# Queueing the merge and modulation steps behind the traced products, with ten weight rows ahead of the merges

## Chip, core and metric

The kernel runs on one NeuronCore of a Trainium2 chip. The metric is the device time of one execution in microseconds (us), shown as the median of several runs; lower is better. One execution was also recorded by the profiler, and all views of the trace come from that one. The engines are named as the profile names them: PE (matrix multiplication), PEld (its weight loads), DVE (vector), ACT (scalar and activation), POOL, and SP, which issues nearly all DMAs. "q" after a name (SPq) means the engine's queue of DMA issues.

## What is computed

One block of an adaptively modulated network on x of shape (4, 1024, 2048), all float32:

```
mod = silu(c) @ wmod                    # 2048 x (6*2048): sections sa, ca, ga, sb, cb, gb
ga, gb = sign(g) * max(|g|, 0.25)
h = layernorm(x) * (1 + ca) + sa
x = x + ga * (causal_conv(h, K) + D*h)  # K: a kernel of 2048 taps from a state-space model, by FFT
h = layernorm(x) * (1 + cb) + sb
x = x + gb * (h @ W.T + bias + sum_e coeffs[e]*scales[e] * (h @ A[e].T) @ Bf[e].T)
```

The reference convolves along the last axis with a 4096-point FFT.

## The kernel before, in words

The kernel has three stages. **Start (0 to about 100 us)**: two sections of the modulation and the table of the convolution kernel K are made. **Convolution (to about 940 us)**: x is taken in 16 groups g of two blocks of 128 rows (r = 0, 1). The convolution is a block-Toeplitz product, done with a three-product scheme ("families" f = 0, 2, 1) with operands split in two float16 parts (`kh`/`kl` and `h`). **Feed-forward (to the end)**: a 2 by 2 Strassen-Winograd product of seven terms, with W and the low-rank update merged beforehand into seven weight matrices `wcd` in DRAM.

In `conv_mm` (L552) the loops run over q = 0, 1 (halves of the output) and r = 0, 1. Each (q, r) does family 0 into a PSUM tile `ya` (pa, L582), ACT copies it to `qs` (L585; the pool has one buffer), family 2 goes into a second tile `yb` (pb, L587), DVE adds `qs` to it (L589), and family 1 accumulates into pa once more (L593), which DVE then multiplies by the gate (L597). A family is 12 products for q = 0 and 24 for q = 1. PSUM tiles come from a pool `acc` of five buffers (ACC = 5, L772), shared with the merges.

The inputs h of group g + 1 are prepared while group g is convolved: statistics on DVE (`stats`, L506), normalising on ACT (L528), transposes on PE into `tp` (L539), modulation on ACT (L542), split on ACT and DVE (L548, L549). After the convolution `conv_post` (L616) stores the rows to `x1d` and takes a second set of statistics. Group 0 is special: its gate is not there until late, so its outputs are gated afterwards in `conv_late` (L608).

Beside this, work that only the feed-forward stage needs is spread through the convolution in small **steps**. A generator `rest()` (L884) hands them out one at a time:

- **rows**: one row block of `wmod`, 1 MB, loaded by SP (`mod_load`, L314, a pool `wm` of three buffers) and multiplied on PE (`mod_mm`, L320, four float32 products, which the trace shows as 8 records named `modps`). Sections 4, 3 and 5 remain for this stage: each has 16 rows and a closing item, 51 items in all. A section's rows accumulate in one PSUM tile, from row 0 to row 15.
- **merges**: first `prep_lora` (L385), which loads A (2 MB, `la`), takes its norms on ACT, loads Bf (2 MB, `lb`) into the same buffer, scales it, and writes it as float16 pairs `lbh` (ACT, L423) and `lbl` (DVE, L424). Then 8 times `merge` (L429), each 15 steps: eight steps of six products `lps` on PE (L448), each with an addition to the loaded weights on DVE (L450), and seven steps of squares, scalings, splits and stores on ACT, DVE and SP (L453 to L495). That makes 121 merge steps.

`rest()` yields two merge steps (MR = 2), then one row, and so on; once the rows are through it still yields an empty step in their place. A last step folds scales (`fold_scale`, L895).

The order: `conv_mm` calls `tick()` after each family, and once more inside each q = 1 family after 12 of its 24 products (L574). So a group has 18 ticks, and a list `PLAN` (L775) says what each does: every tick has one "S", a call of `step()` (L927), which from g = 1 on takes one step from `rest()`. Group 1's first family ends with tick 1, and so on: ticks 1 to 3 belong to (q 0, r 0), 4 to 6 to (q 0, r 1), 7 to 12 to (q 1, r 0), 13 to 18 to (q 1, r 1). This is the order in which the instructions are *traced*. The order in each engine's queue is made afterwards, at build time, by the framework's scheduler: it simulates the engines with its own estimates and lets an instruction that it believes ready overtake earlier traced ones that it believes not ready. On the chip every engine then takes its queue as it stands. DMA issues stand in SP's queue in the same way.

Of the kernel before, what the change touches and what calls it, by code (L numbers as in the profile page):

```python
# [34 lines left out]
class Net:  # L35
# [516 lines left out]
    def conv_mm(self, pl, hs, xs, std, tick, early, out):  # L552

        nc, v = self.nc, self.nc.vector
        gv = None if early else self.gat.rearrange("p (j e t) -> p j e t", e=2, t=P)
        ys = [pl["y"].tile([P, D], F32, tag="y", name="y") for _ in range(2)]
        sums = [pl["sm"].tile([P, 2], F32, tag=f"sums{r}", name="sums") for r in range(2)]
        out[:] = ys, sums

        def family(ps, f, q, r, first):  # L560
            pf = ps.rearrange("p j t -> p (j t)")
            last = 4 * q + 3
            for i in range(last + 1):
                o = P * max(0, i - 4 * q)
                k0 = P * max(0, 4 * q - i)
                c = 2 * i + 2 - f
                h = hs[i // 2][:, :, 4 + i % 2, r] if f == 0 else hs[c // 4][:, :, c % 4, r]
                for x, z in ((0, 0), (0, 1), (1, 0)):
                    nc.tensor.matmul(  # L569
                        pf[:, o:512], h[:, x], self.kf[f][z][:, ds(k0, 512 - o)],  # L570
                        start=first, stop=(i == last and (x, z) == (1, 0)), skip_group_check=True,
                    )
                    first = False
                if i == 3 and q == 1:  # L574
                    tick()

        for q in range(2):
            for r in range(2):
                y = ys[r]
                yv = y.rearrange("p (j e t) -> p j e t", e=2, t=P)  # L580
                jj = slice(4 * q, 4 * q + 4)
                pa = self.acc.tile([P, 4, P], F32, tag="a", name="ya")  # L582
                family(pa, 0, q, r, True)
                qs = pl["q"].tile([P, 4, P], F32, tag="qs", name="qs")
                nc.scalar.copy(qs, pa)  # L585
                tick()
                pb = self.acc.tile([P, 4, P], F32, tag="a", name="yb")  # L587
                family(pb, 2, q, r, True)
                v.tensor_tensor(yv[:, jj, 1, :], pb, qs, ADD)  # L589
                if not early:  # L590
                    v.tensor_tensor(yv[:, jj, 1, :], yv[:, jj, 1, :], gv[:, jj, 1, :], MUL)
                tick()
                family(pa, 1, q, r, False)  # L593
                if early:
                    nc.scalar.copy(yv[:, jj, 0, :], pa)
                else:
                    v.tensor_tensor(yv[:, jj, 0, :], pa, gv[:, jj, 0, :], MUL)  # L597
                    self.residual(xs[r], ys[r], std[:, r : r + 1], sums[r], q)
                tick()
# [168 lines left out]


ORDER = (0, 4, 5, 1, 6, 2, 3)  # L770
MR = 2
ACC, TPS = 5, 2  # L772


# [20 lines left out]
def net(ctx: ExitStack, tc: tile.TileContext, io):  # L795
    nc = tc.nc
    k = Net(ctx, tc, io)
# [18 lines left out]
    def section(sec, pools):  # L816
        for q in range(16):
            if q == 0:
                k.mod_begin()
            k.mod_mm(k.mod_load(pools[q % len(pools)], sec, q), q)  # L820
            yield
        if sec == 0:
            k.sa = k.mod_column(msm, k.kpool, "sa", 0.0)
            k.hinv = k.fold_scale(msm, k.ca, k.sa, "fs1")
        elif sec == 1:
            k.ca = k.mod_column(msm, k.kpool, "ca", 1.0)
        elif sec == 2:
            k.gas, (k.gad,) = k.mod_gate(msm, "gad")
        elif sec == 4:
            k.cb = k.mod_column(msm, k.cst, "cb", 1.0)  # L830
        elif sec == 3:
            k.sb = k.mod_column(msm, k.cst, "sb", 0.0)
        else:
            _, k.gbd = k.mod_gate(msm, "gbd", io["bias"])
        yield
# [4 lines left out]
    def merges():  # L840
        k.prep_lora(pl["lora"], pl["mrg"])
        yield
        for c in range(HC):
            yield from k.merge(pl["lora"], pl["mrg"], c)

    mer = merges()
# [23 lines left out]
    n = 0  # L870
# [12 lines left out]
        pl[name] = pool(left, "p1" + name, bufs)  # L883
    def rest():  # L884
        mods = (x for sec in (4, 3, 5) for x in section(sec, (wmp,)))
        n = 0
        for _ in mer:
            yield
            n += 1
            if n % MR == 0:  # L890
                next(mods, None)
                yield
        for _ in mods:
            yield
        k.ginv = k.fold_scale(msm, k.cb, k.sb, "fs2", k.winv)  # L895
        yield

    fill = rest()
    p2l = ExitStack()
    pr, wc, lf = {}, {}, {}  # L900
# [15 lines left out]
    def early():  # L916
        right.close()
        for name, bufs in (("l", 8), ("t", 1), ("s", 1), ("x2", 1)):
            pr[name] = pool(p2, "p2" + name, bufs, "right")
# [5 lines left out]
        return k.left(pr, u, lf[u])  # L925

    def step():  # L927
        if g >= 1 and "l" not in pr and next(fill, 0) == 0:
            early()

    def post(g, r):
# [10 lines left out]
    for g in range(16):  # L942
# [5 lines left out]
        if g == 15:  # L948
            while "l" not in pr:
                step()  # L950
            load_w(0, ORDER[0])
            lgen = next_left(0)
        plan = iter(PLAN)

        def tick():
            for a in next(plan):
                if a == "S":
                    step()
                    take(lgen, 1)
                elif a == "O":  # L960
                    take(prs.pop(g), 1)
                elif a == "P" and g > 1:
                    post(g - 1, 1)
                elif a == "Q" and g:
                    done[g] = cur
                    post(g, 0)
                elif a == "T" and 0 < g < 15:
                    stats(g + 1)
                elif a == "N" and g < 15:
                    if g + 1 not in prs:  # L970
                        prs[g + 1] = prep(g + 1)
                    take(prs[g + 1], 1)
# [103 lines left out]
```

## Time and profile before

| | |
|---|---|
| runs of the kernel before | median 2165.51 us of 3 (2163.79, 2165.51, 2169.34) |
| the profiled execution | 2160.88 us, of which the span of the trace is 2159.1 us |
| PE | busy 2070.2 us, 96% of the span |
| DVE, ACT | busy 1273.2 us (59%) and 912.2 us (42%) |
| mean granted PE clock | 0.982 |
| DMA | 483.00 MB, mean 224 GB/s |

PE's time by form, from the page's groups: 5376 products of the feed-forward stage (`fX`, `fY`, `fZ`, L712) take about 1200 us; 3456 of the convolution (`ya`, `yb`, L569) about 950 us of counted time, records overlapping; 768 records of rows (`modps`, L322) 116.5 us; 384 of merges (`lps`, L448), 256 of them 87.2 us; the transposes (`tp`) the rest.

How to read the views: a line of the timeline gives the start, the duration, the engine, the line of the kernel, the operation, output<-inputs, how many instructions were taken together, and in brackets the idle time before it with what ended it. A line of the waits gives who waited for whom, the total in us, the number of times and the longest. A line of the windows gives for a stretch of time the busy us of each engine (with the number of instructions), the granted clock, the busy share of the 16 DMA engines and GB/s.

### The profile page before, as it was taken

The page shows a single profiled execution, that of the slowest core. Times are in us where ns is not written, and L with a number is a line of the kernel's source. Part 1 is how long each engine was busy: PE and PEld are TensorE (multiplying, and loading weights), DVE is VectorE, ACT ScalarE, POOL GpSimd, SP SyncE. Part 2 cuts the span into 40 slices and gives each one's busy share as a digit, 9 for nine tenths or more (in the row PEclk, how much of TensorE's full clock was granted, in tenths as well). Part 3 has the DMA queues.
Part 4 walks back from the last instruction along what each step waited for, and adds up shares of the span by engine and source line. Part 5 has one row for each costly group of instructions (what it writes and reads, how often), then busy time and mean ns, then how long its engine had stood idle before and what let it go on. Part 6 is the DMA issues. An engine that isn't in the chain of part 4 may idle for free.

```text
span 2159.1 us, 27722 instructions
## 1 busy us (share of the span) xinstructions
PE 2070.2 (96%) x11084; PEld 1020.6 (47%) x11084; DVE 1273.2 (59%) x2037; ACT 912.2 (42%) x1267; POOL 2.7 (0%) x12
## 2 busy tenths in 40 slices
PE   5696999999999999999999999999999999999999
PEld 1143554545445555654555555545444444444444
DVE  6537778887788877765666566565533323232323
ACT  1246666666667666654555454554200000000000
POOL 0000000000000000000000000000000000000000
PEclk8797999999999999999999999999999999999999
DMA  9987577876775442397556465465695545555542
GB/s 399 379 294 292 209 284 277 306 260 246 280 293 183 173 158 98 127 360 275 218 214 217 173 225 214 169 244 192 248 345 183 185 156 171 169 165 167 175 153 72
DMA packets 127130, 483.00 MB, mean 224 GB/s; under 512 B 13670, under 2 KB 13799, under 8 KB 96023
## 3 DMA queue, kind: packets, MB, share of 16 engines
q1 hardware_dynamic: 126464, 479.65, 61.7%
q8 instruction: 87, 1.43, 0.3%
q10 hardware_dynamic: 538, 1.59, 0.2%
q14 instruction: 41, 0.34, 0.0%
HBM read 325.89 MB, written 155.30 MB: 223 GB/s over the span
## 4 chain that ended last, share of the span: by engine, by line
PE 62%; issue 25%; DVE 7%; DMA 3%; ACT 3%; SPq 0%; POOL 0%; POOLq 0%; DVEq 0%; ACTq 0%
PE fZ L712 23%; PE fX L712 15%; PE fY L712 15%; PE ya L569 3%; PE tp L662 3%; PE yb L569 2%; PE modps L322 1%; DVE h L549 1%; ACT x L622 1%; DVE y L604 1%; ACT h L548 1%; DMA xo<-x1d 1%; DVE s4wr L177 1%; DMA w<-wcd 1%; DVE st L513 1%
## 5 line engine op out<-in xcount | busy, mean ns | idle before, releaser
L712 PEld LDWEIGHTS <-lf 128*128 128x128 f16 x5376 | 525.8, 98 | 620.2 <-issue 0.5
L712 PE MATMUL fZ<-w,lf 128*128 128x512 f16 x2304 | 514.0, 379 | 0.2 <-ACT p L720 0.2
L569 PEld LDWEIGHTS <-h 128*128 128x128 f16 x3456 | 319.7, 98 | 317.1 <-issue 69.1
L569 PE MATMUL ya<-kh,h 128*128 128x512 f16 (+3 forms) x1536 | 380.5, 328 | 8.2 <-ACT qs L585 5.1
L712 PE MATMUL fY<-w,lf 128*128 128x512 f16 x1536 | 343.1, 379 | 0.0
L712 PE MATMUL fX<-w,lf 128*128 128x512 f16 x1536 | 342.5, 379 | 0.0
L569 PE MATMUL ya<-kl,h 128*128 128x512 f16 (+3 forms) x768 | 251.5, 328 | 0.0
L731 DVE SCALAR_TENSOR_TENSOR xo<-xo,mv,gb 128x512 f32<-128x512 f32 x128 | 95.2, 750 | 248.7 <-DMA xo<-x1d 236.7
L569 PE MATMUL yb<-kh,h 128*128 128x512 f16 (+3 forms) x768 | 192.2, 326 | 0.0
L720 ACT COPY p<-fZ 128x512 f32<-128x512 f32 x64 | 37.3, 582 | 292.5 <-PE fZ L712 275.0
L322 PE MATMUL modps<-wm,sct 128*32 128x512 f32 x768 | 116.5, 677 | 43.1 <-DMA wm<-in_wmod 34.0
L664 ACT ACTIVATE gt<-tp,sb,cb 128x256 f32<-128x256 f32 x256 | 123.9, 570 | 63.7 <-PE tp L662 62.1
L720 ACT COPY p<-fX 128x512 f32<-128x512 f32 x32 | 18.7, 586 | 303.9 <-PE fX L712 240.2
L542 ACT ACTIVATE t<-tp,sa,ca 128x256 f32<-128x256 f32 x256 | 126.2, 565 | 32.3 <-PE tp L539 23.4
L549 DVE TENSOR_TENSOR h<-t,h 128x1536 f16<-128x1536 f32 x64 | 112.2, 1754 | 28.2 <-ACT h L548 27.7
L569 PE MATMUL yb<-kl,h 128*128 128x512 f16 (+3 forms) x384 | 125.2, 326 | 0.0
L548 ACT CAST h<-t 128x1536 f16<-128x1536 f32 x64 | 94.1, 1470 | 26.2 <-DVE t L547 26.2
L736 DVE TENSOR_TENSOR fin<-fX,gb 128x512 f32<-128x512 f32 x32 | 22.1, 692 | 125.8 <-PE fX L712 125.7
L448 PE MATMUL lps<-lbh,lac 128*128 128x512 f16 x256 | 87.2, 382 | 6.4 <-ACT lbh L423 5.1
L675 DVE TENSOR_TENSOR lf<-gt,lf 128x1024 f16<-128x1024 f32 x64 | 76.7, 1220 | 18.3 <-ACT lf L674 18.2
L513 DVE BATCH_NORM_STATS2 st<-x 128x6 f32<-128x512 f32 x128 | 83.3, 681 | 5.1 <-DMA x<-in_x 5.1
L539 PE MATMUL tp<-ident,x 128*128 128x128 f32 x512 | 73.0, 279 | 12.8 <-ACT t L542 6.9
(236 smaller groups left out, 1863.1 us busy)
## 6 DMA issues: line engine op xcount, KB each, us to landing
wm<-in_wmod SPq DMA_DIRECT2D x96, 1024.0 KB
lfd<-lf SPq DMA_DIRECT2D x112, 512.0 KB
lf<-lfd SPq DMA_DIRECT2D x112, 512.0 KB
x<-in_x SPq DMA_DIRECT2D x32, 1024.0 KB
x1d<-y SPq DMA_DIRECT2D x32, 1024.0 KB
x<-x1d SPq DMA_DIRECT2D x32, 1024.0 KB
xo<-x1d SPq DMA_DIRECT2D x128, 256.0 KB
out<-xo SPq DMA_DIRECT2D x128, 256.0 KB
```

What stands on the lines that cost most here:

```text
L322: self.last = self.nc.tensor.matmul(self.modps[32 * g : 32 * g + 32, :], self.sct[:, j].rearrange("p r b -> p (r b)"), w[:, ds(512 * g, 512)],
L448: nc.tensor.matmul(ps, la[:, x, k, h], y[:, k, osl], start=(n == 0), stop=(n == 5))
L513: v.bn_stats(st[:, q], xs[r][:, ds(512 * q, 512)])
L539: nc.tensor.transpose(tp[:, c, r], xs[r][:, ds(P * (4 * k + 2 * i + c), P)], self.ident)
L542: nc.scalar.activation(t[:, 2 * i + c], tp[:, c], AF.Identity, bias=self.sa[:, d, b : b + 1], scale=self.ca[:, d, b : b + 1],)
L548: nc.scalar.copy(h[:, 0], t)
L549: v.tensor_tensor(h[:, 1], t, h[:, 0], SUB)
L569: nc.tensor.matmul(pf[:, o:512], h[:, x], self.kf[f][z][:, ds(k0, 512 - o)], start=first, stop=(i == last and (x, z) == (1, 0)), skip_grou ...
L664: nc.scalar.activation(t[:, c0 + c], tp[:, c], AF.Identity, bias=self.sb[:, c0 + c, b : b + 1], scale=self.cb[:, c0 + c, b : b + 1],)
L675: v.tensor_tensor(hl[:, :, 1, :], s, hl[:, :, 0, :], SUB)
L712: nc.tensor.matmul(ps[name], lf[i][:, k, x, :], wc[i][k // 4][:, k % 4, y, :], start=(first and n == 0), stop=(n == 3 * HC - 1), skip_grou ...
L731: v.scalar_tensor_tensor(x, x, m, self.gbias[:, h], ADD, ADD)
```

## The change

Three edits. (1) `conv_mm` keeps the last traced product in `self.cv`. (2) `step()` takes its step inside `tc.issue_after(k.cv.ins)`: each instruction of the step that runs on PE gets an edge that puts it behind that product in PE's queue. It is an order of issue alone, with no semaphore; instructions of the step on DVE, ACT, SP and POOL get no edge. When there is a step and when `early()` is called stays as it was. (3) `rest()` begins with ten rows of section 4 (MOD0 = 10), with `prep_lora` after the first two of them; and then one row follows each three merge steps instead of each two (MR = 3).

```diff
@@ family() in conv_mm, L568
                 for x, z in ((0, 0), (0, 1), (1, 0)):
-                    nc.tensor.matmul(
+                    self.cv = nc.tensor.matmul(
@@ L771
-MR = 2
+MR, MOD0 = 3, 10
@@ rest(), L884
         mods = (x for sec in (4, 3, 5) for x in section(sec, (wmp,)))
+        for n in range(MOD0):
+            if n == 2:
+                next(mer)
+                yield
+            next(mods)
+            yield
         n = 0
         for _ in mer:
@@ step(), L927
-        if g >= 1 and "l" not in pr and next(fill, 0) == 0:
+
+        with tc.issue_after(k.cv.ins):
+            more = g == 0 or "l" in pr or next(fill, 0) is None
+        if not more:
             early()
```

## Prediction

> **What bounds the kernel now.** I read the page's slices first, then the windows, then PE's timeline in the worst window, then its waits, and last SP's queue there. The slices:
>
> ```profile
> PE   5696999999999999999999999999999999999999
> ...
> PEclk8797999999999999999999999999999999999999
> ```
>
> From slice 5 on PE is busy nine tenths or more: PE sets the time, and a change that keeps PE's work (this one removes no product) can only gain idle PE time or lost clock. Idle time stands mainly in slices 1 to 4. The windows show what of it lies where this change reaches, from g = 1 on (about 167 us):
>
> ```profile
> 160.00:180.00 20.00, 17.86 (x116) 9.83 (x114) 18.02 (x25) 13.08 (x19) 0.00 (x0) 1.00 0.96 379
> 180.00:200.00 20.00, 2.13 (x3) 0.39 (x4) 14.13 (x44) 17.88 (x21) 0.40 (x1) 0.52 0.85 335
> 200.00:220.00 20.00, 20.00 (x101) 9.98 (x100) 12.09 (x19) 9.04 (x10) 0.00 (x0) 0.88 0.28 106
> 240.00:640.00 400.00, 391.36 (x2421) 201.34 (x2422) 330.79 (x576) 267.27 (x364) 0.00 (x0) 1.00 0.76 279
> 640.00:760.00 120.00, 113.24 (x693) 63.30 (x691) 107.63 (x201) 84.86 (x113) 0.38 (x1) 1.00 0.52 191
> 762.00:900.00 138.00, 135.13 (x856) 79.56 (x855) 102.13 (x192) 88.35 (x121) 0.00 (x0) 1.00 0.32 115
> ```
>
> PE does 2.13 us of work from 180 to 200. Elsewhere in the convolution it idles 2 to 6% (8.6 us of 400, 6.8 of 120, 2.9 of 138). One hole is the prize. PE's timeline and waits in it:
>
> ```profile
> 174.93 0.22 PE L569 MATMUL ya<-kh,h 128*128 128x128 f16 x1
> 175.08 2.78 PE L322 MATMUL modps<-wm,sct 128*32 128x512 f32 x24
> 192.81 1.92 PE L322 MATMUL modps<-wm,sct 128*32 128x512 f32 x2 [14.95 <-DMA wm<-in_wmod]
> 199.79 0.58 PE L448 MATMUL lps<-lbh,lac 128*128 128x512 f16 x1 [5.06 <-ACT lbh L423]
> 200.17 0.63 PE L569 MATMUL ya<-kh,h 128*128 128x512 f16 x1
> ```
>
> The reader is to see the order. At 174.93 ends (q 0, r 0) of group 1, tick 3. The 24 records are rows 0 to 2 of section 4, which are traced at ticks 3, 6 and 9; two records of row 3 (tick 12) follow; then one product of the first merge; and only then the first product of (q 0, r 1), which is traced before nearly all of them. It uses the same h as r = 0, has no idle time of its own before it, and starts right behind the first `lps`. So the scheduler believed it blocked until that `lps`. My reading (inferred: the trace shows an order, not a reason) is that PSUM tiles of `acc` are handed out in traced order: the first `lps` is traced at tick 2, before r = 1's `ya`, so `ya` waited for a merge whose operand `lbh` comes out of `prep_lora` at 199.8. To fill the time the scheduler pulled up rows; but row 3's load could be asked for late. SP's queue:
>
> ```profile
> 170.50 0.38 SPq L407 DMA_DIRECT2D lb<-in_BfT  x1
> 176.07 4.59 SPq L618 DMA_DIRECT2D x1d<-y  x2
> 180.76 2.56 SPq L502 DMA_DIRECT2D x<-in_x  x2
> 183.41 1.47 SPq L317 DMA_DIRECT2D wm<-in_wmod  x3
> ```
>
> **The hole's worth.** Idle 14.95 + 5.06 = 20.0 us. The clock is granted at 0.52 in it and still at 0.88 over 200:220, which costs (1 - 0.88) x 20 = 2.4 us of PE work. Together 22.4 us, the most that closing it can give.
>
> **The change, part by part.** (a) *Ten rows first.* Merges now begin at step 12 of group 1, the last tick of (q 1, r 0), so no `lps` tile is traced before the `ya`s of (q 0, r 1) and (q 1, r 0); these need only h, complete at 182.8 (DVE L549 starts its last at 181.04) for q = 1 and earlier for q = 0. (b) *issue_after*: rows can't be pulled up, so products aren't behind a row that has not landed unless traced so. PE's work in order, from the end of (q 0, r 0), today 175.1: rows 0 and 1 now stand inside it, at 1.00 us a row ("PE modps L322 x8 1.00" in the chain of work): 177.1. Three families of 12 at 1.63 (today's 209.38 to 211.01): 4.9. Two and a half families of 24 at 4.22 (chain): 10.6. Rows 2 to 8: 7.0. PE reaches row 9 at 199.6 if nothing is late.
>
> What is late next: the rows. DMA was busy 0.94 of the time from 158 to 198 and 0.00 from 198 to 204 (windows), so by 198 rows 0 to 5, A, Bf and g's x and x1d transfers had all moved. Rows 6 to 9 are four loads of 1.05 MB more; at the best rate that the windows show, 420 GB/s (20 to 40 us), 2.5 us each: row 9 lands at 208.0. PE waits 208.0 - 199.6 = **8.4 us** in all, in front of several rows. A second wait hides in the first: family 1 of r = 1 needs `qs` free, which DVE releases at 184.45 (L589, 183.76 + 0.69), against PE's arrival near 182; ACT is in a 1.99 us `lb` scaling then, so 3 to 5 us, during which DMA catches up.
>
> The first `lps` comes at about 209 + 1, today's `lbh` is there at 199.8: covered by 10 us. If `prep_lora`'s loads slip that cover is used up (rival C). The wait of 8.4 us lets the clock drop again; between nothing and the 2.4 of today I take 1, since the pieces are shorter than today's 15. **Sum: 22.4 - 8.4 - 1 = 13 us gained.**
>
> Here a rule of the Trainium skill speaks against the change. TensorE: Matmul & The Clock Gate, section "HAM oscillation — how this bites in real kernels": short PE bursts of some 2 us between DMA waits of 3 to 5 us make the clock fall back each time. Ten rows one by one behind short families are that pattern if every row waits; the 0.52 of this trace agrees that waiting costs clock. By the rule an estimate would have four waits (rows 6 to 9) each followed by up to 3.4 us at half speed, 4 x 1.7 = 6.8 us instead of my 1.
>
> (c) *One row per three merge steps.* Steps: 10 + 1 + 120 + 40 rows + 1 + 1 = 173 instead of 121 + 60 + 1 = 182; the nine missing ones were empty and cost no engine anything. Merges are three of four steps instead of two of three, so DVE's load a group rises: merges are about 166 us of DVE from 200 to 725 (sum of its groups at L424 to L493), 20.8 each; a group takes 0.8 of a merge today, 0.9 then. With 28.9 for the convolution (102.13 x 39.1/138), that is 45.6 us and then 47.6, in a group of some 52 us. DVE stays below PE. Bounds: a gain of the 6.8 us idle in 640:760, where merges today run without rows and DVE stands at 0.90, against a loss at that window's rate (5.6%) over the 458 us that merges will last, 25.7 less today's 15.4, so 10. I take 0, as the row that it is nearest to (240:640, DVE 0.83) idles 2% and the row-less end disappears. (d) *Loads of later rows*: one a group of four steps, about 11.6 us, with three buffers; today one in 8.7 us is not waited for after 230. Nothing. SP: row loads now wait on SP for a row queued behind products, and the `x1d` stores and x loads may stand behind them; that is inside the DMA bound above if it lasts under 8 us. (e) The feed-forward stage needs nothing of this before g = 15: no change.
>
> The profiled execution took 2160.9 (span 2159.1, 1.8 around it), so it would be 2147.9; the median of the runs is 4.6 above it: 2165.5 - 13 = **2152.5**.
>
> **Rivals.** **B, rows are not late**: the row loads move up in SP's queue to 171 and later, before the stores at 176, and PE never waits for more than a `qs`. For it: rows 0 and 1 end by 175, so their buffers are free. Against: DMA is full either way. 2165.5 - 22.4 = 2143. **C, the hole moves to prep_lora**: its loads are traced two rows later; from `lb`'s scaling (182.87) to the first `lps` (199.79) is a chain of 17 us. If `lb` lands after 210 - 17 = 193, the first `lps` waits, and by the PSUM order products behind it too. With `lb` last of all, at 208, the wait is 15 us: 2165.5 - 13 + 15 = 2167.5; halfway 2160. Against it: today SP issues `la` early (151.87) because nothing blocks it, and that stays so. **D, slower**: tied pieces no longer fill while a product waits. Place: family 1 of each (q, r), which waits for the one `qs` copy and, before it, DVE; four a group, 36 over nine groups. Price: one DVE piece of a merge, 1.22 us (L476) each. PE's timeline shows seven such waits today, 0.36 to 2.82 us. It decides from 11 waits on, where it eats the 13 us; at half of the 36 it costs 22: 2165.5 - 13 + 22 = 2174. Against it: with no pieces at all, 762:900, PE idles only 2%. That issue_after does nothing is a part of A: the ten rows alone would still take the `lps` tile away.
>
> **How the numbers follow.** A measurement of this kernel tells 0.3%, 6.5 us, from no change: faster is under 2159, slower over 2172. A (forecast, 2147 to 2158) 0.50; B 0.17; C 0.20, a fifth of it still faster; D 0.13. Faster 0.49 + 0.17 + 0.04 = 0.70, same 0.17, slower 0.13. The range keeps A, B's price with a little of the smaller idle stretches, and C: 2141 to 2168; D lies outside.
>
> **What would show it.** Right: 180:200 with PE above 12 us; the first `ya` of (q 0, r 1) near 178 instead of 200.17; rows of section 4 one by one between families; PE waits for `wm` of 5 to 11 us in all before 212 and none of 15; the first `lps` after 205 without a long wait for `lbh`. Wrong: the `ya` still at 195 or later (my reading of the PSUM order), a wait for `lbh` over 5 us (C), idle time in 240:640 above 20 us (D).

## The result, and the profile after

The changed kernel takes 2172.12 us (median of 20 runs, 2168.04 to 2176.34), the kernel before 2163.21 us (20 runs beside them, 2157.34 to 2169.34). The ratio is 1.004, with a 95% interval of 1.0032 to 1.0049: **0.4% slower**, where 2152.5 us and a gain were predicted. The profiled execution of the changed kernel took 2168.04 us (span 2166.3), 4 us under its median, so the two traces lie 7.2 us apart and the medians 8.9.

The slices of the page of the changed kernel:

```profile
span 2166.3 us, 27709 instructions
...
PE   5698899999999899999999999999999999999999
...
PEclk8799999999999999999999999999999999999999
```

Slice 4, a 6 before, is an 8; slice 5, a 9 before, is an 8 now too. Windows of the changed kernel (length; busy us of PE, PEld, DVE, ACT and POOL; granted clock; DMA share; GB/s):

```profile
160.00:180.00 20.00, 19.40 (x113) 9.88 (x112) 16.83 (x24) 11.61 (x17) 0.00 (x0) 1.00 0.63 222
180.00:200.00 20.00, 19.91 (x125) 9.57 (x124) 18.19 (x45) 5.91 (x10) 0.00 (x0) 1.00 1.00 392
200.00:220.00 20.00, 12.34 (x63) 4.04 (x61) 4.68 (x17) 19.29 (x21) 0.40 (x1) 0.74 0.99 374
220.00:240.00 20.00, 14.00 (x65) 5.69 (x66) 14.36 (x19) 11.06 (x14) 0.00 (x0) 0.83 0.65 247
```

The hole at 180:200 is closed: PE 19.91 us busy there instead of 2.13. But 200:240, where PE was busy all of 40 us before, now holds 26.34 us (12.34 + 14.00). **The hole has moved by 20 us.** What stands in it, in the changed kernel's PE timeline:

```profile
200.36 0.22 PE L569 MATMUL ya<-kh,h 128*128 128x128 f16 x1
202.86 0.44 PE L539 MATMUL tp<-ident,x 128*128 128x128 f32 x2 [2.27 <-ACT x L528]
...
209.66 1.54 PE L539 MATMUL tp<-ident,x 128*128 128x128 f32 x6 [3.41 <-ACT x L528]
...
226.00 0.61 PE L448 MATMUL lps<-lbh,lac 128*128 128x512 f16 x1 [6.44 <-ACT lac L436]
```

The reader is to see what is missing. Between the last product of (q 1, r 0) at 200.36 and the first `lps` at 226.00 stands not one product of the convolution, only rows and transposes. The first product of (q 1, r 1) comes at 226.82, right behind the `lps` products. That is the picture of before with another pair: there (q 0, r 1) stood behind the first `lps`, traced at tick 2; here (q 1, r 1) does, since the first `lps` is now traced at tick 12. And the `lps` itself is 26 us later than before, because its operands are: `lac`, on which it waits last, stands in ACT's queue behind `lbh`. SP's queue of the changed kernel:

```profile
158.45 0.45 SPq L394 DMA_DIRECT2D la<-in_A  x1
162.03 16.10 SPq L317 DMA_DIRECT2D wm<-in_wmod  x3
178.23 3.84 SPq L618 DMA_DIRECT2D x1d<-y  x2
182.16 2.53 SPq L502 DMA_DIRECT2D x<-in_x  x2
184.74 0.78 SPq L407 DMA_DIRECT2D lb<-in_BfT  x1
```

Two more rows stand ahead of `la`, which is issued at 158.45 instead of 151.87. Three row loads stand between `la` and `lb`, as before, but they go later: the last only when its buffer is free, at about 178 (row 1's products, which hold a `wm` buffer, end at 176.67 + 1.07). About then the buffer that `lb` shares with `la` is free too (ACT reads `la` until 178.25), but two stores and two loads of x come first. So `lb` is issued at 184.74 instead of 170.50, 14.2 us later. On ACT its scaling stands behind a norm of the next group (L528, at 200.71), for whose statistics ACT waits 6.7 us, and begins at 202.71 (before 182.87). It then shares ACT with that group's norms and modulation (L542), and the first `lps` follows 23.3 us later instead of 17.

**The ledger.** Comparing the start of the k-th `qs` copy in both traces: (q 1, r 0) of group 1 is 24.8 us earlier than before, the first copy of group 2 is 2.5 us *later*. So 27.3 us are given back at once. In this stretch PE idles 13.7 us (40 - 26.34) and loses some 6 to the low clock (0.26 x 12.34 + 0.17 x 14.00 = 5.6, the busy time of each window times what the grant lacks); in the same stretch of the kernel before, 217.0 to 250.6, it loses neither. The other 7 to 8 are work that now lies here: 30 more records of rows, 15 of merges and 5 of transposes, 7.8 us by their time at full clock.

This hole alone does not make the kernel slower than before. From 160 to 240 PE idles 14.4 us against 20.0 (windows above and in the prediction), and the clock takes 5.6 against some 3.4: the change is still ahead by about 3 us. It falls behind later, here the kernel before and then the changed one:

```profile
240.00:940.00 700.00, 680.99 (x4228) 368.78 (x4229) 572.42 (x1018) 470.46 (x637) 0.38 (x1) 1.00 0.62 229
240.00:940.00 700.00, 672.94 (x4157) 366.13 (x4156) 567.88 (x1009) 468.13 (x639) 0.38 (x1) 0.99 0.58 215
```

Idle 19.0 and 27.1 us: 8 more, and some 2 more of lost clock. The difference between the `qs` copies swings on the way and ends at 7.5 us.

### The profile page after: what moved, and what is told of

Its sections match the earlier page's. It is cut to its first block, busy times and chain, and to the rows that moved or that the text cites. A ratio compares the mean times of both kernels' runs of the same rounds, so it can differ in the third digit from the quotient of the medians.

```text
span 2166.3 us, 27709 instructions
## 1 busy us (share of the span) xinstructions
PE 2075.1 (96%) x11084; PEld 1020.0 (47%) x11084; DVE 1274.6 (59%) x2037; ACT 911.1 (42%) x1267; POOL 2.7 (0%) x12
## 4 chain that ended last, share of the span: by engine, by line
PE 65%; issue 23%; DVE 5%; ACT 4%; DMA 3%; ACTq 0%; SPq 0%; POOL 0%; POOLq 0%; DVEq 0%
PE fZ L712 23%; PE fY L712 15%; PE fX L712 15%; PE ya L569 4%; PE tp L662 3%; PE yb L569 2%; PE modps L322 1%; DMA wm<-in_wmod 1%; ACT t L542 1%; DVE h L549 1%; ACT x L622 1%; DVE st L513 1%; ACT h L548 1%; ACT x L528 1%; PE tp L539 0%
## 5 line engine op out<-in xcount | busy, mean ns | idle before, releaser
L542 ACT ACTIVATE t<-tp,sa,ca 128x256 f32<-128x256 f32 x256 | 125.3, 566 | 30.9 <-PE tp L539 22.6
```

The source lines that it names most:

```text
L542: nc.scalar.activation(t[:, 2 * i + c], tp[:, c], AF.Identity, bias=self.sa[:, d, b : b + 1], scale=self.ca[:, d, b : b + 1],)
```

## The experiments

Theory 1: products wait for `acc` tiles handed out in traced order, so that a first `lps` without its operands blocks the products traced behind it; the changed kernel makes these operands late. Rivals: the denser merges of MR = 3; the load of the rows on the DMA engines; `issue_after` by itself. Ratios are to the kernel before, measured beside each run on the same chip; the medians of runs on different chips differ by a little more or less than their ratios.

**1. The queueing alone.**

```diff
-MR, MOD0 = 3, 10
+MR, MOD0 = 2, 0
```

> The changed kernel with MR = 2 and MOD0 = 0: issue_after alone. Theory 1 (PSUM tiles of acc are handed out in traced order, so products traced behind the first lps wait for prep_lora's lbh, wherever that lps is traced): the first lps is traced at tick 2 again, so PE's hole stands again from about 175 to 200 us, now without the three rows in it; the time is that of before plus 0 to 5 us. Theory 2 (issue_after itself costs: tied pieces no longer fill while a product waits): at least 6 us slower than before, with the loss spread over 240 to 760 us.

2166.69 us; 1.0024 (1.0011 to 1.0036). PE's timeline, this run:

```profile
201.17 0.59 PE L448 MATMUL lps<-lbh,lac 128*128 128x512 f16 x1 [23.65 <-ACT lbh L423]
```

Rows no longer move up into the hole, and it is one wait of 23.65 us for `lbh`. The wait for a row, 14.95 us before, was never the cause: it stood in front of the wait for `lbh`.

**2. The rows alone**: `step()` as before, without `issue_after`.

> The changed kernel without issue_after: ten rows first, prep_lora after two, MR = 3. Theory 1: (q 0, r 1) and (q 1, r 0) of group 1 run early, and the hole stands again in front of the first lps near 205 to 226 us, as in the changed kernel; the time is within 4 us of the changed kernel, 2168 to 2176. Theory 2: the loss came from the ties, so this one is at or below before, 2155 to 2164.

2166.10 us; 1.0018 (1.0007 to 1.0029), a little under what was expected. `lb` is issued at 188.72, the first `lps` comes at 229.92: the second hole belongs to the ten rows, not to the queueing.

**3. prep_lora ahead of the ten rows.**

```diff
-            if n == 2:
+            if n == 0:
```

> The changed kernel with prep_lora ahead of the ten rows instead of after two. Theory 1: lb is issued some 10 us earlier than 184.7 and the first lps starts near 212 to 217 instead of 226; 8 to 12 us faster than the changed kernel, 2160 to 2164. Theory 2: no difference from the changed kernel, 2170 to 2174.

2159.65 us; 0.9994 (0.9983 to 1.0004): 12 us under the changed kernel, 10 by the ratios. `lb` is issued at 172.62, and the first `lps` waits for nothing at 223.20. What is left between 200 and 224 is rows and x that land late. This run's PE timeline and windows of 4 us:

```profile
201.42 1.06 PE L322 MATMUL modps<-wm,sct 128*32 128x512 f32 x8 [1.36 <-DMA wm<-in_wmod]
204.06 1.58 PE L322 MATMUL modps<-wm,sct 128*32 128x512 f32 x8 [1.58 <-DMA wm<-in_wmod]
206.57 1.94 PE L322 MATMUL modps<-wm,sct 128*32 128x512 f32 x8 [0.92 <-DMA wm<-in_wmod]
211.33 0.69 PE L539 MATMUL tp<-ident,x 128*128 128x128 f32 x2 [2.83 <-ACT x L528]
```

```profile
200.00:204.00 4.00, 1.13 (x12) 0.16 (x8) 2.91 (x7) 4.00 (x4) 0.00 (x0) 1.00 0.94 336
204.00:208.00 4.00, 3.02 (x16) 0.36 (x16) 4.00 (x2) 3.63 (x4) 0.00 (x0) 0.56 1.01 426
208.00:212.00 4.00, 1.17 (x6) 0.29 (x2) 1.40 (x11) 3.02 (x3) 0.00 (x0) 0.50 1.03 424
```

The DMA engines are full here (0.94 to 1.03), and the granted clock is 0.56 and 0.50 from 204 on, after the first two of these waits.

**4. prep_lora traced ahead of group 0's convolution.** Its step is taken out of the ten rows and stands as `next(mer)` before the loop over g.

> The changed kernel with prep_lora traced before group 0's convolution and out of rest(). Theory 1: lbh is there before 200, the first lps does not wait and the hole is gone at both places; 15 to 22 us faster than the changed kernel, 2150 to 2157, unless the 4 MB of loads delay section 2's rows in group 0 by as much (then PE waits for wm between 110 and 160). Theory 2: no difference from the changed kernel.

2167.85 us; 1.0022 (1.0011 to 1.0034): a miss. SP's queue holds one line of 15 row loads from 140.47 that lasts 48.10 us, the stores and x loads stand behind it, and the first `lps` comes at 225.68. `lbh` is ready by 149, as was meant, but now the rows themselves clog the queue, and x is asked for at 194.00 instead of 182.93 in run 3. In 200:220 PE is busy 15.38 us, more than in run 3 (11.46); the rest of this run's loss lies elsewhere and was not taken apart.

**5. The kernel before, with a PSUM buffer for `lps` alone**, taken from `acc`.

```diff
+        self.lpp = ctx.enter_context(tc.tile_pool(name="lpp", bufs=1, space=PSUM))
...
-                ps = self.acc.tile([P, 512], F32, tag="a", name="lps")
+                ps = self.lpp.tile([P, 512], F32, tag="p", name="lps")
...
-ACC, TPS = 5, 2
+ACC, TPS = 4, 2
```

> The kernel before, with lps in a PSUM pool of its own of one buffer and acc cut from five to four. Theory 1 (order of PSUM tiles): the first ya of (q 0, r 1) in group 1 no longer stands behind the first lps and starts before 186 us instead of 200.2; 8 to 18 us faster than before, less what the missing acc buffer costs in the other groups. Rival (it was held by something else, such as an evacuation or h): it starts near 200 as before, and the time is that of before or worse.

2151.91 us; 0.9946 (0.9933 to 0.9959). PE's timeline of this run (its lines are one higher from L42 on):

```profile
178.85 0.39 PE L570 MATMUL ya<-kh,h 128*128 128x512 f16 x1
...
187.27 0.38 PE L570 MATMUL ya<-kh,h 128*128 128x512 f16 x1 [3.14 <-DVE y L590]
...
204.64 0.38 PE L449 MATMUL lps<-lbh,lac 128*128 128x512 f16 x1 [0.77 <-ACT lbh L424]
```

(q 0, r 1) begins at 178.85, not at 200.17, and `lps` keeps its place behind `lbh`. Nothing of the rows or of `prep_lora` was moved.

**6. Its control: `acc` with four buffers and nothing else.**

> Control: the kernel before with acc cut from 5 buffers to 4 and nothing else. Theory 1: the own buffer's 11.7 us came from the order of the tiles, so four buffers alone gain nothing: 2163 to 2170. Rival (fewer buffers help by themselves): 2152 to 2158.

2170.02 us; 1.0032 (1.0019 to 1.0045). The rows' wait in the hole is 15.70 us again and `lps` comes at 203.99. So four buffers cost 7 us, and the own buffer is worth not 11.7 but some 18 (2170.0 - 2151.9). The pool that `lps` shares is shown as the cause of the hole. That its tiles go in traced order fits both holes: each time the pair traced next behind the first `lps` is held.

**7. The changed kernel with that buffer.**

> The changed kernel with lps in a PSUM buffer of its own (acc cut from 5 buffers to 4). Theory 1 (the products of (q1, r1) traced behind the first lps can't start before that tile is handed out, and the changed kernel's lb comes late): the second hole at 200 to 226 fills with products of (q1, r1), and the time falls by 8 to 14 us against the changed kernel, to 2158 to 2164. Rival (the ten rows and the DMA queue set the end, not the order of the tiles): it stays within 4 us of the changed kernel, 2168 to 2176.

2162.32 us; 0.9992 (0.9981 to 1.0003), 9.8 under the changed kernel. Its windows:

```profile
200.00:220.00 20.00, 19.85 (x127) 9.37 (x125) 6.49 (x22) 16.75 (x21) 0.40 (x1) 1.00 0.81 289
220.00:240.00 20.00, 13.81 (x68) 5.80 (x67) 14.48 (x19) 15.80 (x18) 0.00 (x0) 0.83 0.90 364
```

PE is busy 19.85 of the 20 us at 200:220, with `lb` as late (185.68) as in the changed kernel. The second hole has the same cause as the first in this stretch. In 220:240 PE is no busier than in the changed kernel (14.00): there it waits 3.6 us for a row and 2.6 for `lac`.

**8. to 10. MR**: the kernel before with MR = 3; the changed kernel, and run 3, with MR = 2.

> The kernel before with MR = 3 alone: one row per three merge steps. Theory A (denser merges cost PE waits from 240 to 780 us): the hole at 175 to 200 stays and 3 to 7 us are lost after it. Theory B (the spacing costs nothing): within 2 us of before.

> The changed kernel with MR = 2 instead of 3; ten rows first and issue_after stay. Theory A: 3 to 7 us faster than the changed kernel, 2165 to 2169, with the second hole at 200 to 226 unchanged. Theory B: 2170 to 2174.

> The changed kernel with prep_lora ahead of the rows and MR = 2. Theory A: the two repairs add up, 2153 to 2157. Theory B: as prep_lora first alone, 2158 to 2161.

MR = 3 alone: 2160.53 us, 0.9987 (0.9978 to 0.9995). MR = 2 in the changed kernel: 2177.72 us, 1.0067 (1.0053 to 1.008). MR = 2 in run 3: 2169.05 us, 1.0025 (1.0014 to 1.0036), against 0.9994. The rival of the denser merges falls: MR = 3 helps in all three. One place could show why. The last row is handed out after 102 of 121 merge steps in the kernel before, after 83 in the changed kernel with MR = 2, and not before the merges end with MR = 3; what follows the last row are merges without rows. The stretch 640:800, first the changed kernel with MR = 2, then the kernel before with MR = 3 (152.05 us busy in the kernel before):

```profile
640.00:800.00 160.00, 143.64 (x840) 79.67 (x841) 137.04 (x249) 108.52 (x149) 0.38 (x1) 0.97 0.51 185
```

```profile
640.00:800.00 160.00, 155.53 (x984) 83.05 (x982) 126.13 (x240) 95.25 (x128) 0.38 (x1) 1.00 0.62 225
```

Idle: 16.4, 8.0 and 4.5 us. That does not settle it: the changed kernel, with no merges left over, idles 9.5 us there.

**11. MR = 3 on top of run 5.**

> The kernel before with lps in a PSUM buffer of its own and merges in threes (MR=3), no ten rows and no issue_after. If the two gains measured alone (11.7 us and 2.8 us) add: 2148 to 2150, faster than both kernels. If merges in threes gained only by the hole that the own buffer has filled: 2151 to 2154.

2158.82 us; 0.9977 (0.9966 to 0.9988): worse than run 5 by 7 us, outside both expectations. Here the denser merges do cost: idle PE in 240:640 rises from 7.8 to 13.5 us. The sign of MR depends on the arrangement; why is open.

**12. Run 3 without the queueing.**

> The run with prep_lora ahead of the ten rows, without issue_after. If queueing the ticks behind the last traced product costs by itself the 5 us that two pairs of runs show: 2153 to 2157. If it only costs by making prep_lora late: no difference, 2158 to 2162.

2154.21 us; 0.9953 (0.9937 to 0.9969), against 0.9994. The queueing costs 5 us by the medians and 9 by the ratios, beside ten rows whose order it was meant to keep. From 240 to 940 PE idles 24.9 us with it and 16.5 without. PE's waits for the one `qs` copy make 5.1 of these 8.4; here first run 3, then this run (total, times, longest):

```profile
PE ya L569 <- ACT qs L585: 6.6, 9, 2.0
```

```profile
PE ya L569 <- ACT qs L585: 1.5, 6, 0.4
```

From the changed kernel to run 2, the other pair that differs in the queueing alone, it is 7.9 us in nine waits against 2.1 in seven.

**13. and 14. Where the queueing costs**: run 3 with `issue_after` in groups 0 to 2 only, and in groups 3 and later only.

> The run with prep_lora ahead of the ten rows, with the queueing behind the last traced product in groups 0 to 2 only. If its 5 us are the waits of ya for qs that grew from 1.5 to 6.6 us behind 240 us (queued steps no longer move up into them): nearly all of it lies behind group 2, so 2153 to 2156, with qs waits of about 1.5 to 3 us. Rival (it costs in groups 1 and 2, where the rows and merges stand): 2157 to 2162.

> The other half: the queueing in groups 3 and later only. By the first theory 2157 to 2161, with qs waits of 5 us or more behind 240 us; by the rival 2153 to 2156.

Groups 0 to 2: 2155.18 us, 0.9964 (0.9951 to 0.9976). Groups 3 and later: 2159.30 us, 0.9984 (0.9975 to 0.9992). The waits behind 240 us, in this order:

```profile
PE ya L569 <- ACT qs L585: 1.6, 6, 0.4
```

```profile
PE ya L569 <- ACT qs L585: 8.3, 8, 2.1
```

The price lies in groups 3 and later, and the waits for `qs` go with it: a family that must wait for the one `qs` copy has nothing beside it when the pieces traced behind it may not move up. The two intervals just touch; the waits point the same way. In run 1, with MR = 2 and no rows ahead, these waits are no longer than in the kernel before (5.5 us in seven, 5.1 in eight), and the hole idles longer instead (23.65 us, not 20.0). So this price is shown for the kernels with ten rows and MR = 3 alone.

**15. All that gained, together**: the rows and MR = 3, `prep_lora` ahead of them, no queueing, `lps` in its own buffer.

> All that has gained, together: the ten rows and MR=3 with prep_lora ahead of them, no queueing, and lps in a PSUM buffer of its own (acc 4). If the own buffer and the early prep_lora fill the same stretch, the sum doesn't add: 2150 to 2158, no better than the own buffer alone. If the rows bring work of their own into it: 2143 to 2149.

2150.34 us; 0.9937 (0.9923 to 0.9951). This run's window:

```profile
200.00:220.00 20.00, 20.00 (x126) 7.41 (x124) 12.13 (x26) 13.34 (x9) 0.00 (x0) 1.00 0.87 308
```

No row is waited for. It beats both kernels, but is no better than the own buffer alone by more than the intervals (0.9923 to 0.9951 and 0.9933 to 0.9959): the two fill the same stretch.

**16. The own buffer taken from the transposes** (`ACC, TPS = 5, 1`).

> The kernel before with lps in a PSUM buffer of its own, taken from the transposes (tps from 2 buffers to 1) and not from acc, which stays at 5. Four buffers of acc alone cost 7 us: if that price can be saved, 2145 to 2150. If one buffer for the transposes makes each wait for the eviction of the last: slower than the kernel before, 2166 or more.

2204.16 us; 1.019 (1.0175 to 1.0204). 180:240 is as full as wished (58.2 of 60 us), and the feed-forward stage pays: its transposes wait 15.1 us for ACT's eviction (`gt`, 13 times) instead of 0.9. These waits are less than half of the loss. For the same 11084 instructions PE counts 2112.9 us of busy time instead of 2070.2; why is open.

## Why the prediction was wrong, step by step

- *The hole's worth, 22.4 us*: right in kind and size. It closed (idle 0.7 us in 160:200 instead of 20.0), and (q 1, r 0) came 24.8 us earlier.
- *The reading that `acc` tiles go in traced order*: right, and borne out by runs 5 to 7. The prediction drew half of its consequence. It moved the first `lps` to tick 12 and named the families traced ahead of it; those *behind* it, (q 1, r 1), it left to half a sentence of rival C.
- **The step that failed**: "The first `lps` comes at about 209 + 1, today's `lbh` is there at 199.8: covered by 10 us." `lbh`'s cast began at 220.36, and the first `lps` came at 226.00. It took 199.8 from a trace in which `prep_lora` is the first step and used it for a kernel in which it is the third, though `la` and `lb` then stand behind more row loads in SP's queue. Part (d) saw that the x1d stores and x loads may stand behind a blocked row load; that `lb` stands behind all of them was priced only as rival C. Putting `prep_lora` first again (run 3) gives 10 to 12 us back.
- *Rival C, the hole moves to prep_lora, 0.20*: this is what happened. Its extreme, 2167.5, stands against 2172.1; it priced the lateness at 15 us, and run 3 gets 10 to 12 back. Its counter-argument, "today SP issues `la` early (151.87) because nothing blocks it, and that stays so", was false: `la` went 6.6 us and `lb` 14.2 us later. Its chain of 17 us became 23.3, since ACT now has the next group's norms and modulation between the scaling and the first `lps`.
- *Rows late, 8.4 us*: near in sum, but not for rows alone. In the changed kernel only 0.9 us in 200:226 is a wait for a row; 5.7 are for x and 6.4 stand in front of `lps`. In run 3, where `prep_lora` is early, the three waits for rows are 3.9 us and the two for x, which shares the full DMA engines, 4.1; all idle time of 200:220 there is 8.5.
- *Cooling, 1 us*: too small. The clock was 0.66 in 200:220 of run 3, which costs 0.34 x 11.46 busy us = 3.9 us; in the changed kernel 5.6 in 200:240. The estimate of 6.8 us by the Trainium skill, TensorE: Matmul & The Clock Gate, section "HAM oscillation — how this bites in real kernels", was too large for run 3, by about as much as the 1 was too small. Its rule, that waits of over some 3.4 us are what makes the clock fall, is not what run 3 shows: the grant was 0.56 in 204:208 after waits of only 1.36 and 1.58 us.
- *issue_after does nothing of its own (a part of A)*: the other step that failed, a term put at nothing. It costs 5 us by the medians and 9 by the ratios (run 3 against run 12), 5 to 6 in the changed kernel (against run 2). Rival D had the mechanism, pieces that no longer fill while a product waits for `qs`, and priced it at 36 waits x 1.22 = 44, or half of it. Measured: nine waits instead of six, 5.1 us more; against the kernel before the changed one has nine instead of eight, 2.8 us more, and its idle time in 240:640 is 16.5 us, under the 20 that the prediction set as D's sign. That 2167.5 + 5 meets the time measured is in part luck, since C's 15 us was too much.
- *MR = 3 costs nothing*: mis-sized. It gains 2.8 us alone and 6 to 9 with the ten rows, inside the bound of 6.8 but for the last; with the own buffer it loses 7, inside the bound of 10.

With both failures taken away, in run 12, the time is 2154.21 us, near the forecast of 2152.5. That is luck in part: its idle time and lost clock from 160 to 240 are some 14 us where the forecast had 9.4, and MR = 3 was put at nothing.

By parts, from the ratios: MR = 3 gains 0.13%; the ten rows with `prep_lora` behind two of them turn this into a loss of 0.18%; the queueing makes it 0.40%. What stays open: the waits behind 240 us other than those for `qs`, and the sign of MR.

## What to carry to other kernels

Where two streams of work share one pool of buffers, find the first tile of the stream that may be late and list everything traced behind it: moving that tile later only changes what is caught behind it, while a pool of its own (here one buffer) sets it free, and a control tells what the lost buffer costs. A step that is put ahead of another also puts its loads ahead in the DMA queue, and a load that waits for a buffer holds back every load behind it, so the ready time of an operand must be worked out again from the new queue, not taken from the old trace. Small pieces that may move up are worth more than their order: before tying them to a place, count the short waits that they fill.

## What the runs showed of the hardware

The granted clock fell to half after waits much shorter than those in the kernel before (1.36 and 1.58 us in run 3, against one of 14.95), and stayed at 0.50 to 0.56 over 204:216 though PE worked 6.9 of these 12 us. In the changed kernel it held at 1.00 over 200:204 and 204:208, where PE worked 1.73 and 1.35 us, with waits of 2.27 and 0.90; what decides is not shown. In 200:220 of run 3 the waits cost 8.5 us in idle time and some 4 us more in clock.
